# A fixed instruction order for four engines in the delta rule's products, with head norms summed in pairs

## The chip, the cores and the metric

The kernel runs on one core of a Trainium2 chip. Its engines are TensorE (PE, with its weight loads shown as PEld), VectorE (DVE), ScalarE (ACT), GpSimd (POOL) and SyncE (SP), which only issues DMAs here. The metric is the device time of one execution in microseconds (us), lower is better. The median of three runs of the kernel before is 2903.06 us (2902.81 to 2907.43).

## The reference

A block of three layers on 128 sequences of 32 tokens, width 512, in float32: `x = x + cross_attention(layernorm(x))`, then a delta-rule layer, then a feed-forward layer with Hadamard rotations and quantised weights. The change lies in the delta-rule layer, which computes per sequence:

```python
h = rms(layernorm(x), attn_norm_w)
q, k, v = (silu(silu(causal_dwconv(h @ W.T, conv))) for each)    # 4 taps along the tokens
q, k = l2norm(q), l2norm(k)                 # per head: 32 heads of 16
beta = sigmoid(h @ Wbeta.T)
for t in range(32):                         # the delta rule, S is 16x16 per head
    err = S @ k[t] - v[t]
    S = S - beta[t] * outer(err, k[t])
    o[t] = S @ q[t]
x = x + rms(o, out_norm_w) @ Wout.T
x = x + (silu(h2 @ Wgate.T) * (h2 @ Wup.T)) @ Wdown.T     # h2 = rms(x, mlp_norm_w)
```

The recurrence over 32 tokens is solved without a state: the products of all keys with all keys and queries of a sequence are formed first, a triangular system is solved by substitution over the tokens, and the result is multiplied by the masked query products.

## The kernel before

The program has four stages: cross attention; the **delta products** (`delta_products`); the **MLP stage** (`delta_out_mlp`), which finishes the delta layer and does its MLP; and the last feed-forward layer.

`delta_products` works in eight **rounds**, one per group of 512 rows (16 sequences). A round has twelve **steps** (`j` = 0 to 11): `k` and `q` for each of four 128-channel pieces in turn, then `v` for the four pieces. The last round goes through `k`, then `v`, then `q`.

In every step `channels` lets PE multiply the normed rows `hT` (transposed) with 128 columns of a weight into the PSUM bank `pp` (three of them), ACT scales it with the last tap into `acc` (three), and DVE adds the other three taps. One step later `activated` lets ACT apply Silu twice into `kq` or `v2`. The rest of a round is spread over the steps:

- `square` and `add`: squares of `k` and `q` (ACT), summed per head on PE into `sums` with the 0/1 matrix `hs`. `add` also multiplies `hT` with `wb` for the logits of beta.
- `lengths`: ACT takes Tanh and Sqrt of `sums`. In the next round `by_tokens` (step 1) turns them on PE, and DVE makes the norms `n` and `beta`; `put_q` and the `inverted` steps write the query norms (`rq`); `put_v` (steps 2 to 5) turns `v2` on PE, scales it on DVE into `vt` and writes it (`vd`).
- `products`: for each **piece** (128 channels by 256 rows; eight in a round) SP first loads `kqm`, a copy of `k` and `q` masked by head, with eight DMAs (`masked_operand`, three buffers, `hold` decides when). `multiply` then does sixteen small matmuls into two `pg` banks, ACT copies them to `kk` (six buffers), POOL writes `ld`, multiplies with the causal mask and writes `pd`. `due` lists the steps in which a piece is multiplied.
- `load`, `normed`: the next round's rows (`xt`, three buffers) are loaded, normed on DVE to `hn` (two buffers) and turned by PE and ACT into the next `hT`.

**Substitution** (`Substitution.solve`) works on the groups that are finished: DVE alternates a product `pr` and a subtraction from `W`, 31 times with falling length, 128 x 1984 elements at first. It loads `L` (one buffer, four loads) and `W` (two buffers) on SP and writes `ud` on POOL. `mixed` interleaves its steps with a round's by costs: a solve counts 90, `LANDING` (8) of it for the loads, and each round from the second gets `SHARE` (0.27 of a solve); the rest runs beside the MLP stage.

The order of instructions on PE and ACT is fixed in this stage to the order in which the program issues them, by the wrapper `InOrder`, which ties each instruction to the one before. DVE, SP and POOL are ordered by the scheduler, which may move a ready instruction ahead of others.

Ahead of round 0, `scaled_rows` multiplies the rows of `wk`, `wq`, `wv` and `wb` with `norm_w` on DVE, and POOL clears the operands `um` and `pe` that the MLP stage fills later. DVE clears `kqm` in the first steps.

Of the kernel before, what the change touches and what calls it, by code (L numbers as in the profile page):

```python
# [494 lines left out]
def scaled_rows(nc, wp, name, norm, ws, engine=None):  # L495

    mul = engine.mul if engine else nc.vector.tensor_scalar_mul
    nw = wp.tile([P, DC], FP, name=name, bufs=1)
    nc.sync.dma_start(nw, norm.rearrange("(c p) -> p c", p=P))
    for t in ws:  # L500
        for dc in range(DC):
            mul(t[:, dc, :], t[:, dc, :], nw[:, dc : dc + 1])


class Substitution:
# [4 lines left out]
    def __init__(self, g, pool, ld, vd, ud):  # L510
        self.nc, self.pool, self.ld, self.vd, self.ud = g.nc, pool, ld, vd, ud

    def solve(self, gi):
# [5 lines left out]
        def load(s):  # L519
            nc.sync.dma_start(  # L520
                L[:, s : s + some].rearrange("p s h t -> p s (h t)"), rows[:, s : s + some]
            )
# [3 lines left out]
        nc.sync.dma_start(  # L526
# [5 lines left out]
        for s in range(T):  # L532
            if s % some == 0 and s + some < T:
                load(s + some)
            nc.vector.tensor_mul(w[:, s], w[:, s], bc(W[:, s, :, HD], HD))
            n = T - 1 - s
            if n:
                pr = self.pool.tile([P, T - 1, H4, HD], FP, name="pr")
                nc.vector.tensor_mul(  # L539
                    pr[:, 0:n],  # L540
                    bc(L[:, s, :, s + 1 : T].rearrange("p h t -> p t h"), HD),
                    w[:, s].unsqueeze(1).to_broadcast([P, n, H4, HD]),
                )
                yield 0.3 + 0.07 * n
                nc.vector.tensor_sub(w[:, s + 1 :], w[:, s + 1 :], pr[:, 0:n])  # L545
# [7 lines left out]
def masked_operand(nc, m, kq):  # L553


    for h in range(HH):
        rows = slice(h * HD, (h + 1) * HD)
        nc.sync.dma_start(m[rows, h % H4], kq[rows])  # L558
# [31 lines left out]
def inverted(nc, rq, r):  # L590
# [3 lines left out]
    nc.sync.dma_start(r, every)  # L594
    yield
    nc.vector.tensor_scalar_max(r, r, 1e-12)
    nc.vector.reciprocal(r, r)
# [4 lines left out]
def delta_products(  # L602
    g: Ctx, x1, stats, norm_w, wqT, wkT, wvT, conv_q, conv_k, conv_v, wbT, heads, causal, ld, vd,
    pd, rq, kd, beside,
# [16 lines left out]
    act = InOrder(tc, nc.scalar)  # L621
    with stack:
# [13 lines left out]
        scaled_rows(nc, wp, "nw", norm_w, [w["k"], w["q"], w["v"], w["b"]])  # L636

        kqm = [wp3.tile([P, H4, 2, KT], FP, name=f"kqm{i}") for i in range(3)]
        blank = [t[:, h] for t in kqm for h in range(H4)]
        mv, rs = stats  # L640

        def load(n):
            xt = xp.tile([P, D], FP, name="xt")
            nc.sync.dma_start(xt, x1[n * P : (n + 1) * P, :])
            return xt

        def normed(n, xt, hT):

            i = n % GT
            hn = hp.tile([P, D], FP, name="hn")  # L650
            nc.vector.tensor_scalar(
                hn, xt, mv[:, n, 0:1], rs[:, n, 1:2], ALU.subtract, ALU.mult
            )
            act.copy(hT[:, :, i * P : (i + 1) * P], g.transposed(ps, hn, g.ident, pe=pe))

        def channels(hT, n, ec):
# [9 lines left out]
            for d in range(1, TAPS):  # L666
                last = nc.vector.scalar_tensor_tensor(  # L667
# [3 lines left out]
            return acc.rearrange("p b t -> p (b t)"), last.ins  # L671
# [16 lines left out]
        def hold():  # L688
            while len(held) < min(len(pieces), count["done"] + len(kqm)):
                gi, ec, half, kq = pieces[len(held)]  # L690
                m = kqm[len(held) % len(kqm)]
                masked_operand(nc, m, kq[:, :, half * KT : (half + 1) * KT])
# [13 lines left out]
        class Group:  # L706

            def __init__(self, gi):  # L710
                self.gi = gi
                self.sums = psn.tile([3 * H, SG], FP, name="pn")
                self.v = {}

            def square(self, kq, of="kq"):
# [3 lines left out]
                return sq  # L719

            def add(self, sq, hT, ec, of="kq"):
                at = dict(start=ec == 0, stop=ec == DC - 1)
                if "k" in of:
                    pe.matmul(self.sums[0:H], hs[:, ec, :], sq[:, 0], **at)
                    pe.matmul(
                        self.sums[H : 2 * H], w["b"][:, ec, :], hT[:, ec, :], **at
                    )
                if "q" in of:
                    return pe.matmul(self.sums[2 * H :], hs[:, ec, :], sq[:, 1], **at)

            def lengths(self, of="kq"):

                if "k" in of:
                    f = self.factors = wk.tile([3 * H, SG], FP, name="f", bufs=1)
                    act.activation(f[H : 2 * H], self.sums[H : 2 * H], AF.Tanh, scale=0.5)
                for n, r in (("k", slice(0, H)), ("q", slice(2 * H, 3 * H))):
                    if n in of:
                        act.activation(self.factors[r], self.sums[r], AF.Sqrt)

            def by_tokens(self):  # L740
                f = self.factors
                pt = ps.tile([P, GT, 2 * H], FP, name="ps")
                for i in range(GT):
                    pe.transpose(
                        pt[:, i, :], f[0 : 2 * H, i * P : (i + 1) * P], g.ident[0 : 2 * H, 0 : 2 * H]
                    )
                self.n = st.tile([P, GT, H], FP, name="n")
                nc.vector.tensor_scalar_max(self.n, pt[:, :, 0:H], 1e-12)
                self.beta = st.tile([P, GT, H], FP, name="beta")
                nc.vector.tensor_scalar(self.beta, pt[:, :, H:], 0.5, 0.5, ALU.mult, ALU.add)  # L750
                n2 = st.tile([P, GT, H], FP, name="n2", bufs=1)
                nc.vector.tensor_mul(n2, self.n, self.n)
                nc.vector.reciprocal(n2, n2)
                nc.vector.tensor_mul(self.beta, self.beta, n2)

            def put_q(self):

                for c in range(DC):
                    rows = slice(2 * H + c * HH, 2 * H + (c + 1) * HH)
# [5 lines left out]
            def put_v(self, ec):  # L765
# [6 lines left out]
                nc.vector.tensor_mul(  # L772
# [13 lines left out]
        def behind_round(old, j):  # L786
# [4 lines left out]
            if j == 1:  # L791
# [3 lines left out]
                    nc, rq[old.gi], st.tile([P, P], FP, name="rl", bufs=1)  # L795
# [9 lines left out]
        due = (0, 1, 1, 0, 1, 1, 0, 1, 1, 0, 1, 1)  # L805
        loads = (2, 3, 4, 8)
# [813 lines left out]
```

## Time and profile before

| | |
|---|---|
| median of 3 runs | 2903.06 us |
| the profiled execution | 2912.17 us |
| its span, first to last instruction | 2910.4 us |
| PE busy | 2815.8 us (97%) |
| DVE busy | 1995.4 us (69%) |
| ACT busy | 1034.9 us (36%) |
| POOL busy | 741.5 us (25%) |
| first `pp` matmul of the delta products | at 686.3 us |
| first `pm` matmul of the MLP stage | at 1215.7 us |

The first rows are device times; the others come from one profiled execution, whose own time is the one to set beside its span. Busy time is a union over an engine's instructions. PE's matmuls are pipelined, so a busy PE need not be at its peak rate; the granted clock (1.00 is full speed) is given beside it in the views by stretch. In the view of waits a line names the waiting engine, tile and line, what released it, the total in us, how often, and the longest. In a timeline a line has start, length, engine, source line, operation and count; the bracket is the idle time before it and what ended it. Helper calls through `InOrder` all stand under L151. Most fp32 matmuls show as two records.

### The profile page before, as it was taken

The numbers are of one execution on the slowest core, as the hardware profiler recorded it, in microseconds if no ns is written. First come the engines' busy times: TensorE is split into PE (matmuls) and PEld (weight loads), VectorE is DVE, ScalarE is ACT, GpSimd is POOL, SyncE is SP. The second block draws the span as 40 slices with busy tenths as digits, with TensorE's granted clock in tenths as the row PEclk, the third lists the DMA queues.
The fourth block names the chain that finished last, engine by engine and source line by source line (L and its number), as shares of the span: only waits on it lengthen the run. The fifth ranks groups of instructions, "written<-read, shape, count | busy, mean of one in ns | idle before, by whom it ended". The sixth has DMA issues, their size and how long they took to land.

```text
span 2910.4 us, 44713 instructions
## 1 busy us (share of the span) xinstructions
PE 2815.8 (97%) x16726; PEld 1676.1 (58%) x16726; DVE 1995.4 (69%) x3355; ACT 1034.9 (36%) x1794; POOL 741.5 (25%) x1102
## 2 busy tenths in 40 slices
PE   8999999997999899999999999999999999999998
PEld 4444444443434344567666767776776756666665
DVE  2453544425599895678787878887722279999997
ACT  1111111213666466522212221211221147677665
POOL 2232323322777677221212111101000000000000
PEclk9999999998999899999999999999999999999999
DMA  9898998873555545841414141413231124444443
GB/s 317 268 321 296 345 334 291 302 248 87 163 161 144 167 135 155 236 137 57 131 57 132 57 132 54 123 59 94 69 112 33 35 73 83 90 88 82 87 81 71
DMA packets 347176, 429.77 MB, mean 148 GB/s; under 512 B 151888, under 2 KB 252624, under 8 KB 344528
## 3 DMA queue, kind: packets, MB, share of 16 engines
q1 hardware_dynamic: 305952, 324.36, 37.0%
q0 software_dynamic: 41008, 102.55, 11.6%
q8 instruction: 133, 2.18, 0.3%
q14 instruction: 83, 0.68, 0.1%
HBM read 288.88 MB, written 94.37 MB: 132 GB/s over the span
## 4 chain that ended last, share of the span: by engine, by line
PE 58%; DVE 11%; issue 2%; DMA 2%; POOL 2%; ACT 1%; SPq 1%; ACTq 0%; DVEq 0%; POOLq 0%
PE ps L151 18%; PE pm L1063 9%; PE pm L1052 9%; PE pm L1055 9%; PE pp L151 4%; PE ps L1026 4%; DVE W L545 3%; DVE acc L667 2%; DVE pr L539 2%; PE ps L995 2%; PE pg L151 1%; POOL kk L583 1%; DMA xs<-x 1%; SPq L558 1%; PE pn L151 1%
## 5 line engine op out<-in xcount | busy, mean ns | idle before, releaser
L1052 PE MATMUL pm<-hT,wg 128*128 128x256 f32 x1408 | 341.1, 385 | 0.2 <-ACT hT L1041 0.2
L1055 PE MATMUL pm<-hT,wu 128*128 128x256 f32 x1408 | 336.4, 382 | 1.8 <-DVE wu L1113 1.3
L539 DVE TENSOR_TENSOR pr<-L,W 128x1984 f32<-128x1984 f32 (+30 forms) x248 | 307.6, 1240 | 8.6 <-DMA L<-ld 4.0
L545 DVE TENSOR_TENSOR W<-W,pr 128x1984 f32<-128x1984 f32 (+30 forms) x248 | 308.1, 1242 | 2.9
L1063 PE MATMUL pm<-wd,mT 128*128 128x512 f32 x704 | 307.4, 592 | 0.0
L1055 PEld LDWEIGHTS pm<-hT,wu 128*128 128x128 f32 x1408 | 269.3, 192 | 39.7 <-DVE wu L1113 1.6
L1052 PEld LDWEIGHTS pm<-hT,wg 128*128 128x128 f32 x1408 | 261.9, 190 | 50.0 <-issue 12.0
L1063 PEld LDWEIGHTS pm<-wd,mT 128*128 128x128 f32 x704 | 132.4, 190 | 160.2 <-issue 160.0
L151 PE MATMUL ps<-wq,qT 128*128 128x512 bf16 x960 | 217.1, 379 | 3.0 <-ACT t L151 3.0
L1057 ACT ACTIVATE sg<-pm 128x256 f32<-128x256 f32 x176 | 67.0, 382 | 325.3 <-PE pm L1052 311.8
L1058 DVE TENSOR_TENSOR mT<-pm,sg 128x256 f32<-128x256 f32 x176 | 73.8, 419 | 156.4 <-PE pm L1055 152.0
L1389 POOL DMA_DIRECT2D xo<-x x31 | 26.3, 849 | 526.1 <-ACT xo L151 491.7
L323 POOL DMA_DIRECT2D vx<-vn x256 | 126.3, 500 | 119.5 <-DVE vn L319 84.3
L151 PEld LDWEIGHTS <-qT 128*128 128x128 bf16 x960 | 94.0, 98 | 103.7 <-issue 3.9
L151 DVE TENSOR_TENSOR mb<-m 128x1024 f32<-128x1024 f32 x128 | 153.2, 1217 | 0.1
L151 DVE TENSOR_TENSOR m<-mb 128x1024 f32<-128x1024 f32 x128 | 150.7, 1219 | 1.2
L579 POOL DMA_DIRECT2D ld<-kk x128 | 93.4, 729 | 151.2 <-ACT kk L151 121.4
L151 ACT ACTIVATE t<-ps,magic,qs 128x512 f32<-128x512 f32 x158 | 115.5, 780 | 46.0 <-DVE qs L151 42.2
L583 POOL TENSOR_TENSOR kk<-kk,cm 128x256 f32<-128x256 f32 x128 | 124.9, 976 | 2.7
L151 PEld LDWEIGHTS ps<-hd,mT 128*128 128x128 f32 x1024 | 120.8, 194 | 6.9 <-ACT mT L151 2.8
L151 PE MATMUL pp<-hT,wk 128*128 128x512 f32 x256 | 122.3, 622 | 1.5 <-DVE acc L667 0.8
L151 PE MATMUL ps<-hd,mT 128*128 128x128 f32 x1024 | 121.3, 277 | 2.3 <-ACT mT L151 2.3
(230 smaller groups left out, 4820.0 us busy)
## 6 DMA issues: line engine op xcount, KB each, us to landing
kall<-in_ctxT_dram SPq DMA_DIRECT2D x32, 2056.0 KB
cx<-in_ctx_dram SPq DMA_DIRECT2D x32, 2048.0 KB
x<-xo POOLq DMA_DIRECT2D x64, 256.0 KB, 3.5
ld<-kk POOLq DMA_DIRECT2D x128, 128.0 KB, 2.6
pd<-kk POOLq DMA_DIRECT2D x128, 128.0 KB, 2.6
L<-ld SPq DMA_DIRECT2D x32, 512.0 KB
pe<-pd SPq DMA_DIRECT2D x256, 64.0 KB
kqm<-kq SPq DMA_DIRECT2D x448, 32.0 KB
```

Of the source, the lines that this page charges most:

```text
L151: got = method(*args, **kw)
L323: nc.gpsimd.dma_start(vx[r : r + T, j, :], vn[j * T : (j + 1) * T, halves[h]])
L539: nc.vector.tensor_mul(pr[:, 0:n], bc(L[:, s, :, s + 1 : T].rearrange("p h t -> p t h"), HD), w[:, s].unsqueeze(1).to_broadcast([P, n, H4, ...
L545: nc.vector.tensor_sub(w[:, s + 1 :], w[:, s + 1 :], pr[:, 0:n])
L579: nc.gpsimd.dma_start(ld[r].rearrange("(i p) f -> p i f", p=P), kk[:, 0].rearrange("p i h t -> p i (h t)"))
L583: nc.gpsimd.tensor_mul(q, q, cm.unsqueeze(1).to_broadcast([P, 2 * H4, T]))
L1026: nc.tensor.matmul(pw, oT[:, i, dc, :], wo[:, dc, :], start=dc == 0, stop=dc == DC - 1)
L1052: nc.tensor.matmul(pg, wg[:, dc, fs], hT[:, dc, :], start=dc == 0, stop=dc == DC - 1)
L1055: nc.tensor.matmul(pu, wu[:, dc, fs], hT[:, dc, :], start=dc == 0, stop=dc == DC - 1)
L1057: nc.scalar.activation(sg, pg, AF.Silu)
L1058: mark[:] = [nc.vector.tensor_mul(mT[:, fc, :], pu, sg).ins]
L1063: nc.tensor.matmul(pd, mT[:, fc, i * P : (i + 1) * P], wd[:, fc, :], start=fc == 0, stop=fc == FC - 1,)
```

## The change

- DVE and SP are wrapped in `InOrder` as well for this stage, so that their instructions, those of the substitution included, run in the order in which the program issues them. POOL is still ordered by the scheduler.
- Within a step `multiply` comes before `activated`, and `due` is shifted by one, so that a piece is multiplied a step later (in round 0 from step 5 on). `normed` goes a step ahead of the transposes, now `turned`; the fourth `xt` is loaded in step 7 instead of 8.
- The sums of squares go into four blocks of 32 rows instead of two: `add` runs twice a round (steps 6 and 10) on two channel pieces at once, one block for each of `k`, `q` and the piece's parity. The logits have a bank and a matmul group of their own (`logits`, 16 matmuls of 128 columns in step 11), and Tanh a tile of its own.
- The four tiles of round 0 are normed and turned before the weights are scaled; `wq` is scaled on ACT.
- `um` and `pe` are cleared on DVE in the first steps of round 0, in twelve pieces after those of `kqm`.
- The last round gets 0.7 of a share of substitution, at the pace of the others, so that its last part has none; `by_tokens` and `put_v` come a step later there.

```diff
-        scaled_rows(nc, wp, "nw", norm_w, [w["k"], w["q"], w["v"], w["b"]])
+    dve = substitution.dve = InOrder(tc, nc.vector)
+    sync = substitution.sync = InOrder(tc, nc.sync)
...
-        blank = [t[:, h] for t in kqm for h in range(H4)]
+        blank = [t[:, h] for t in kqm for h in range(H4)] + blanks
...
+            def add(self, ec, of="kq"):
+                if ec == 0 and "k" in of:
+                    self.sums = psn.tile([4 * H, SG], FP, name="pn")
+                for n in of:
+                    for r in range(2):
+                        at = (2 * "kq".index(n) + r) * H
+                        last = pe.matmul(
+                            self.sums[at : at + H], hs[:, ec + r, :], self.sq[r][:, "kq".index(n)],
+                            start=ec == 0, stop=ec == DC - 2,
+                        )
+                self.sq.clear()
+                return last
+
+            def logits(self, hT):
+                pb = ps.tile([P, P], FP, name="ps")
+                for dc in range(DC):
+                    for i in range(GT):
+                        pe.matmul(
+                            pb[i * H : (i + 1) * H], w["b"][:, dc, :], hT[:, dc, i * P : (i + 1) * P],
+                            start=dc == 0, stop=dc == DC - 1,
+                        )
+                self.tanh = st.tile([P, P], FP, name="tanh")
+                act.activation(self.tanh, pb, AF.Tanh, scale=0.5)
...
-        due = (0, 1, 1, 0, 1, 1, 0, 1, 1, 0, 1, 1)
-        loads = (2, 3, 4, 8)
+        due = (1, 0, 1, 1, 0, 1, 1, 0, 1, 1, 0, 1)
+        loads = (2, 3, 4, 7)
...
-                acc, last = channels(hT, n, ec)
-                with tc.issue_after(last):
-                    for _ in range(min(H4, len(blank))):
-                        nc.vector.memset(blank.pop(0), 0.0)
+                acc = channels(hT, n, ec)
+                for _ in range(min(H4, len(blank))):
+                    dve.memset(blank.pop(0), 0.0)
+                if due[j] and count["done"] < len(held) and (old or j >= 5):
+                    multiply()
                 activated()
                 waiting.append((acc, dst, masked(ec) if n == "q" else kept))
-                if due[j] and count["done"] < len(held) and (old or j >= 4):
-                    multiply()
                 if 3 <= j <= 9 and j % 2:
-                    sq = new.square(kq[(j - 3) // 2])
-                if 4 <= j <= 10 and j % 2 == 0:
-                    new.add(sq, hT, (j - 4) // 2)
+                    new.square(kq[(j - 3) // 2])
+                if j in (6, 10):
+                    new.add((j - 6) // 2)
...
                 if j == 11:
+                    new.logits(hT)
                     new.lengths()
                 if 7 <= j <= 10:
-                    normed((gi + 1) * GT + j - 7, xt[j - 7], hT_next)
+                    turned((gi + 1) * GT + j - 7, hn, hT_next)
+                if 6 <= j <= 9:
+                    hn = normed((gi + 1) * GT + j - 6, xt[j - 6])
...
         for i in range(GT):
-            normed(i, load(i), hT)
+            turned(i, normed(i, load(i)), hT)
+        for n, mul in (
+            ("k", dve.tensor_scalar_mul), ("b", dve.tensor_scalar_mul), ("q", act.mul),
+            ("v", dve.tensor_scalar_mul),
+        ):
+            scaled_rows(mul, w[n], nw)
...
-        for t in (*um, *pe):
-            nc.gpsimd.memset(t, 0.0)
...
-            return [(SHARE, part(all_u, SHARE))] if gi else []
+            return [(SHARE, part(all_u, SHARE * (0.7 if gi == NG - 1 else 1.0)))] if gi else []
```

## The prediction

> **What bounds the kernel now.** I read the page, then the busy time by stretch, which cuts the span into cross attention (0 to 686.3 us), the delta products (686.3 to 1215.7), the MLP stage (to about 2340) and the last FFN. The diff touches only the second. Cutting it at the first `pp<-hT,wk` of each round gives rounds 1 to 6 below (columns: stretch, length, then busy us of PE, PEld, DVE, ACT, POOL, granted clock, DMA share, GB/s).
>
> ```profile
> 744.60:805.90 61.30, 59.26 (x421) 25.55 (x413) 39.48 (x55) 39.49 (x65) 41.92 (x62) 1.00 0.60 171
> 805.90:870.80 64.90, 62.50 (x416) 26.73 (x412) 64.80 (x78) 40.31 (x66) 54.17 (x66) 0.97 0.57 157
> 870.80:936.70 65.90, 63.30 (x417) 26.75 (x413) 65.52 (x93) 40.55 (x66) 49.24 (x66) 0.97 0.53 148
> 936.70:1016.40 79.70, 64.59 (x417) 27.52 (x413) 71.44 (x98) 40.47 (x66) 54.11 (x67) 0.89 0.55 163
> 1016.40:1080.90 64.50, 60.88 (x417) 25.90 (x413) 61.74 (x83) 40.19 (x66) 49.77 (x66) 1.00 0.51 138
> 1080.90:1139.60 58.70, 58.70 (x416) 25.49 (x412) 33.10 (x52) 39.94 (x66) 47.33 (x70) 1.00 0.54 147
> ```
>
> All six do the same matmuls. Round 6 is pure PE: 58.7 us, no wait. Rounds 2 and 3 are pure DVE (64.80 of 64.90), because the substitution ran there as early as it could: by the same view its three lines take 6.9, 36.3, 37.8, 42.6, 33.0 and 0 us in rounds 1 to 6. So DVE is overfull in four rounds and half empty in the sixth. The six take 395.0 us against 6 x 58.7 = 352.2. The waits of the stage show how PE feels it:
>
> ```profile
> PEld pg L151 <- ACT kk L151: 31.0, 28, 4.2
> PE pg L151 <- ACT kk L151: 14.5, 13, 3.3
> PE pg L151 <- DMA kqm<-kq: 11.9, 2, 10.6
> PE ps L151 <- DVE hn L651: 9.9, 1, 9.9
> ```
>
> The PE timeline shows what a wait costs beyond itself: after 2.04 us the next eight `pp` records take 5.40 us (3.60 in round 6).
>
> ```profile
> 804.41 1.55 PE L151 MATMUL pg<-kqm,kq 64*32 64x256 f32 x32 [2.04 <-ACT kk L151]
> 805.90 5.40 PE L151 MATMUL pp<-hT,wk 128*128 128x512 f32 x8
> 974.47 2.82 PE L151 MATMUL pg<-kqm,kq 64*32 64x256 f32 x32 [10.55 <-DMA kqm<-kq]
> ```
>
> The 10.55 us in round 4 is SP's queue: a `W` load for a later group waits until 963.32 with the `kqm` loads behind it.
>
> ```profile
> 952.74 1.33 SPq L520 DMA_DIRECT2D L<-ld  x2
> 963.32 0.32 SPq L526 DMA_DIRECT2D W<-vd  x1
> 963.75 36.67 SPq L558 DMA_DIRECT2D kqm<-kq  x47
> ```
>
> At the front, DVE scales 16 weight pieces before the last two `hn`, slowed to 1.2 us each for `wq` while POOL's memset runs:
>
> ```profile
> 676.00 4.91 DVE L502 TENSOR_SCALAR wq<-wq,nw 128x512 f32<-128x512 f32 x4
> 682.99 0.99 DVE L651 TENSOR_SCALAR hn<-xt,mv,rs 128x512 f32<-128x512 f32 x2
> ```
>
> ```profile
> 675.76 4.08 POOL L1528 MEMSET pe<- 128x2048 f32 x2 [0.43 <-DVE mv L82]
> ```
>
> **The front.** The new order puts `hn` ahead of the scaling, gives `wq` to ACT and the memsets to DVE in round 0. PE's transposes of the first two tiles end at 673.8, which frees their buffers; two `hn` at 0.5 and the last statistics end near 674.5, four `wk` at 0.45 near 676.3. ACT's copies stand behind its table load and two square roots (to 676.3), two at 0.55 end at 677.4. First `pp` near 677.6 instead of 686.3: **-8.7**. Four `wq` on ACT, unseen there, cost between 0.48 (DVE's own) and 0.93 (ACT on 128x768); I take 0.6, 2.4 in all, done at 680 before the first `pp` ends (5.5 us, slow clock as now).
>
> **PE per round.** Before, `add` ran four times: six records (three column groups side by side) in 0.99 us each, so three matmuls cost hardly more than one. After, two times four groups: 1.98 if the fourth also runs beside the others, 3.7 if it does not; I take 1.98, since `ps<-pe,um` (128x32 weights in four groups) does 16 matmuls of 128 columns in 1.01. That row has the shape of `logits`, so 1.01 for it (2.0 if they ran singly, by the transposes' 0.49 for four). The `tanh` transpose adds 0.12. Net 3.96 to 3.11: -0.85, round 6's 58.7 becomes **57.9**.
>
> **DVE per round.** Other work than substitution is 28 to 29 us when DVE is full (64.8 - 36.3 in round 2). The written order spreads substitution over 71 steps, from step 9 of round 1 to step 8 of round 7. Of 156.6 us now, 0.3 of a share leaves (7.3 of 142 cost units, 8 us): 148.5 / 71 = 2.1 a step, 25 a round. With 0.2 to 0.3 for the split `n` (0.28 the whole), 54 us against PE's 57.9. The twelve new memsets (0.485, as the `kqm` ones) fall in round 0, where DVE has 31 of 58 busy; six steps there hold 1.9 of convolution and 1.9 of memset against PE's 3.44, some 2 us of lag, which the `pp` banks cover. ACT loses about 0.9 a round (three 0.59 rows become one and a shorter one).
>
> **The waits.** ACT's `kk` copies now stand before the two Silus of the step; at 933.39 ACT waited 4.26 for `acc` and the copies behind it released PE at 935.21. In the new order they need no convolution newer than two steps. `kqm` has three steps (14 us) instead of two (9.7) for two loads of 8 x 0.59 = 9.4. The early `W` load now comes a round after the `ud` write it waits for. So most of the 47.6 (395.0 - 6 x 57.9) can go. What the fixed queues add: on DVE, convolution 10 of round 1 stands behind the first `W` product, which waits for a load (landing 9.0 us; now 51 us into the round, DVE is there after nine steps of 4.8, one `pp` of 3.44 and 2.6 for `acc` and convolution, 49), some 2 us, which PE's three `pp` banks (14 us) absorb; on SP, `kqm` loads stand behind the second solve's `L` load, which waits for DVE to finish the first, at most a step's DVE work (5 us), again within three steps. I leave 1 us a round, bounds 0 (round 6 now) and 4 (rounds 2, 3, 5 now exceed 58.7 by 6 to 7, mostly DVE): rounds 1 to 6 become 353.4, **-41.6**. POOL: 47.3 without substitution, mean 51.8 with 37.4 of it, so near 50.
>
> **Round 0**: 1.33 of `kqm` wait gone, one product (1.02) moved to the end, `add` and `logits` -0.97: **-3.3**. **Round 7 and the tail** (76.1 to the first `pm`): +1.0 for that product, `add` 4 x 0.98 to 2 x 0.98 plus 1.1, the late `q` sums from four turns to two (-1.9); -1.7 in sum, but `wu`'s load waits on `put_q` there, so **-1**. Bounds 0 and -3. DVE has 46 us busy in these 76 and gets 17 more, none of it in the last third.
>
> **MLP stage**: PE 1113.6 of 1124.3. Substitution ends its second solve about 7.5 us later; its `um` copies end at 1264.9 for matmuls at 1286.9, so it is covered; without that slack up to 3 us. Taken at 0.
>
> Sum: -8.7 - 3.3 - 41.6 - 1 = -54.6. The profiled execution took 2912.17 (span 2910.4), so 2857.6; the median 2903.06 lies 9.1 below it, so 2848.5, say **2849**.
>
> **A rule against it.** POOL's `kk` multiply takes 0.74 alone and up to 2.75; in round 2, full of substitution, 17 took 20.17 us, in round 6 18 took 13.36. The Trainium skill, "SBUF — State Buffer", Who interferes with whom, says that a DVE instruction with two SBUF inputs shuts out a GpSimd instruction that reads SBUF, and the one that starts second waits for all of it. The rows of rounds 2 and 6 agree. By that rule a substitution product in nearly every step could catch nearly every multiply; it gives the third rival.
>
> **Rivals.**
> - *Strict order couples DVE and PE* (or DVE's 54 is really 61): each step waits a little, rounds of 62 rather than 58.9. For it: 93% load and no freedom to fill a gap. Against: three `pp` and `acc` buffers. 6 x 62 = 372, -23 - 13 = -36: 2867. Chance 0.25.
> - *SP's order stalls PE anyway*: loads behind `L`, `W` or `xt` come late some four times, 10.55 each: 42 back, 2891. The later use speaks against it. Chance 0.07.
> - *Slower*: every `kk` multiply is shut out as at worst. Then POOL has 47.3 + 16 x 2.0 = 79 us a round, `kk`'s six buffers fill, and PE waits: 6 x 79 - 395 - 13 = +66, 2969. It decides above (67.9 - 47.3)/16 = 1.29 over 0.74, a mean of 2.0 us; the densest round shows 1.19. With any mix of it and the second rival beyond 55 us of stalls: chance 0.07.
> - *It doesn't do what it says*: fewer matmuls save nothing as they overlapped already. Partly true, and counted; without it -48, 2856, inside the main case.
>
> **Chances.** Main case 0.59, coupling 0.25, SP 0.07, slower 0.07, no change 0.02. The main case alone runs from 2838 (no wait left, tail at its best) to 2860; the range adds the coupling case and its neighbours: 2836 to 2879. A measurement of this kernel can tell about 0.2% (5.8 us) from no change. Faster 0.91, same 0.02, slower 0.07.
>
> **What would show it.** First `pp` near 677.6; rounds 1 to 6 each 58 to 60 us, DVE busy evenly near 54; `pg <- kk` under 10 us and no `kqm` wait above 2; two `pn` groups of 1.0 and one `ps<-hT,wb` of 1.0 a round; MLP stage unchanged. Rounds above 62 with PE waiting for `acc` or `pp` would prove me wrong on DVE, `kk` multiplies near 2 us on POOL.

## The result and the profile after

The changed kernel takes 2875.2 us (median of 4 runs, 2874.1 to 2880.2) against 2905.2 for the kernel before on the same chip (2902.8 to 2911.0): a ratio of 0.9891, 95% interval 0.9876 to 0.9906. So it is 30 us faster where 54.6 were forecast. The profiled execution took 2874.5 us, its span is 2872.8. Cut as in the prediction:

| stretch | before | after | difference | forecast |
|---|---|---|---|---|
| up to the first transposes of the delta products | 672.7 | 667.1 | -5.6 | 0 |
| front: from there to the first `pp` | 13.6 | 4.5 | -9.1 | -8.7 |
| round 0 | 58.3 | 53.6 | -4.7 | -3.3 |
| rounds 1 to 6 | 395.0 | 370.6 | -24.4 | -41.6 |
| round 7 and the tail, to the first `pm` of L1083 | 76.0 | 81.4 | +5.4 | -1 |
| what follows | 1694.7 | 1695.6 | +0.9 | 0 |

The first row is work that the change does not touch; it lay between 665.8 and 672.7 in the profiles of this study. Without it the spans differ by 32.0 us, or 1.1%, as the medians do. Two rows carry the miss: rounds 1 to 6 (17.2 us less gain than forecast) and the tail (6.4 the other way).

Rounds 1 to 7 after, by the busy time by stretch (stretch, length, busy us of PE, PEld, DVE, ACT, POOL, granted clock, DMA share, GB/s):

```profile
725.20:790.00 64.80, 60.97 (x441) 27.27 (x437) 35.92 (x55) 39.83 (x65) 43.65 (x64) 0.95 0.58 167
790.00:850.90 60.90, 58.48 (x442) 25.89 (x438) 58.83 (x69) 39.82 (x65) 51.89 (x66) 1.00 0.52 145
850.90:911.60 60.70, 58.40 (x441) 25.88 (x437) 59.41 (x75) 39.97 (x65) 49.22 (x65) 1.00 0.56 153
911.60:975.70 64.10, 61.28 (x442) 27.19 (x438) 62.40 (x87) 40.06 (x65) 47.95 (x65) 0.95 0.53 144
975.70:1035.90 60.20, 59.23 (x442) 26.36 (x438) 53.83 (x80) 39.76 (x65) 44.98 (x67) 1.00 0.69 207
1035.90:1095.80 59.90, 58.35 (x442) 25.86 (x438) 57.51 (x71) 39.82 (x65) 51.05 (x65) 1.00 0.61 173
1095.80:1177.20 81.40, 73.33 (x453) 34.35 (x449) 70.85 (x103) 51.23 (x84) 50.69 (x73) 0.97 0.72 204
```

The rounds are even now, but none is at the pace of 57.9 that the prediction worked out for PE. DVE is busy for 97% of rounds 2 to 4 (58.83 of 60.90, 59.41 of 60.70, 62.40 of 64.10), not for 93%, and for 70.85 us of the tail's 81.4 where it had 46.0 before. The view of waits for this stage shows what became of PE's waits:

```profile
PE ps L151 <- DVE hn L151: 9.9, 11, 2.8
PE ps L97 <- DVE y L1071: 4.8, 1, 4.8
PE ps L151 <- DVE W L151: 3.8, 1, 3.8
```

The lines `pg <- ACT kk` (14.5 us) and `pg <- DMA kqm` (11.9) are gone from PE. What stands there instead is `hn`: the transposes of the next group's tiles in steps 7 to 10 wait for VectorE. The `W` line is one of them too, its releaser being the instruction just ahead of `hn`. The PE timeline has the two largest, and what follows each:

```profile
781.12 1.09 PE L151 MATMUL ps<-ident,hn 128*128 128x128 f32 x4 [3.83 <-DVE W L151]
782.00 6.05 PE L151 MATMUL pp<-hT,wv 128*128 128x512 f32 x8
...
951.54 1.11 PE L151 MATMUL ps<-ident,hn 128*128 128x128 f32 x4 [2.82 <-DVE hn L151]
952.45 6.16 PE L151 MATMUL pp<-hT,wv 128*128 128x512 f32 x8
```

The eight `pp` records behind each of them take over 6 us instead of 3.60, and the granted clock of these two rounds is 0.95. In round 1 that comes on top of the wait; in round 4 it cost nothing, as a run further down shows. In round 1, DVE in turn waited for the tile's load, and SP shows why: the load of `xt` stands in the written order behind the first solve's `L` and `W`, and the tile was there 8.5 us after its issue.

```profile
780.43 0.55 DVE L151 TENSOR_SCALAR hn<-xt,mv,rs 128x512 f32<-128x512 f32 x1 [6.19 <-DMA xt<-x]
```

```profile
769.72 0.39 SPq L151 DMA_DIRECT2D L<-ld  x1
770.32 1.52 SPq L151 DMA_DIRECT2D W<-vd  x1
771.93 0.44 SPq L151 DMA_DIRECT2D xt<-x  x1
```

### The profile page after: what moved, and what is told of

Same layout as the page of the kernel before. It is cut to its first block, busy times and chain, and to the rows that moved or that the text cites. A ratio compares the mean times of both kernels' runs of the same rounds, so it can differ in the third digit from the quotient of the medians.

```text
span 2872.8 us, 45044 instructions
## 1 busy us (share of the span) xinstructions
PE 2793.6 (97%) x16863; PEld 1675.9 (58%) x16926; DVE 2016.4 (70%) x3371; ACT 1037.3 (36%) x1791; POOL 728.4 (25%) x1098
## 4 chain that ended last, share of the span: by engine, by line
PE 59%; DVE 13%; issue 2%; DMA 1%; SPq 0%; ACT 0%; POOL 0%; DVEq 0%; POOLq 0%; ACTq 0%
PE ps L151 19%; PE pm L1083 10%; PE pm L1086 9%; PE pm L1094 9%; PE pp L151 5%; PE ps L1057 4%; DVE acc L151 3%; PE ps L1026 2%; DVE W L151 2%; DVE pr L535 1%; DVE W L541 1%; DVE pr L151 1%; PE pg L151 1%; DMA xs<-x 1%; DVE m L151 1%
## 5 line engine op out<-in xcount | busy, mean ns | idle before, releaser
L1083 PE MATMUL pm<-hT,wg 128*128 128x256 f32 x1408 | 342.5, 385 | 0.2 <-ACT hT L1072 0.2
L1083 PEld LDWEIGHTS pm<-hT,wg 128*128 128x128 f32 x1408 | 262.5, 191 | 50.3 <-issue 10.0
L535 DVE TENSOR_TENSOR pr<-L,W 128x960 f32<-128x960 f32 (+30 forms) x201 | 238.4, 1186 | 7.6 <-DMA L<-ld 3.8
L541 DVE TENSOR_TENSOR W<-W,pr 128x1024 f32<-128x1024 f32 (+30 forms) x202 | 241.3, 1195 | 2.3
L151 PE MATMUL ps<-wq,qT 128*128 128x512 bf16 x930 | 217.2, 381 | 4.6 <-ACT t L151 3.0
L151 PEld LDWEIGHTS <-qT 128*128 128x128 bf16 x960 | 94.4, 98 | 105.0 <-issue 6.1
L151 DVE TENSOR_TENSOR mb<-m 128x1024 f32<-128x1024 f32 x128 | 153.3, 1219 | 0.1
L151 DVE TENSOR_TENSOR m<-mb 128x1024 f32<-128x1024 f32 x128 | 150.8, 1220 | 1.2
L151 ACT ACTIVATE t<-ps,magic,qs 128x512 f32<-128x512 f32 x158 | 115.6, 780 | 42.7 <-DVE qs L151 38.9
L151 PEld LDWEIGHTS ps<-hd,mT 128*128 128x128 f32 x1024 | 120.8, 194 | 6.9 <-ACT mT L151 2.8
L151 PE MATMUL ps<-hd,mT 128*128 128x128 f32 x1024 | 121.3, 277 | 2.3 <-ACT mT L151 2.3
L151 PE MATMUL pp<-hT,wv 128*128 128x512 f32 x256 | 120.3, 614 | 0.0
L579 POOL TENSOR_TENSOR kk<-kk,cm 128x256 f32<-128x256 f32 x128 | 118.4, 925 | 2.7
L151 PE MATMUL pp<-hT,wk 128*128 128x512 f32 x256 | 116.2, 596 | 1.9 <-ACT hT L151 1.9
```

Source lines behind the costliest of these rows:

```text
L151: got = method(*args, **kw)
L535: self.dve.tensor_mul(pr[:, 0:n], bc(L[:, s, :, s + 1 : T].rearrange("p h t -> p t h"), HD), w[:, s].unsqueeze(1).to_broadcast([P, n, H4, ...
L541: self.dve.tensor_sub(w[:, s + 1 :], w[:, s + 1 :], pr[:, 0:n])
L579: nc.gpsimd.tensor_mul(q, q, cm.unsqueeze(1).to_broadcast([P, 2 * H4, T]))
L1083: nc.tensor.matmul(pg, wg[:, dc, fs], hT[:, dc, :], start=dc == 0, stop=dc == DC - 1)
```

## The experiments

The question was where 17 us of rounds 1 to 6 and 6 us of the tail went. Theory A: the order. `hn` stands in DVE's written order only one step ahead of the transposes that need it, behind a step's convolution and substitution, so PE waits as soon as DVE is a step late. The main rival, called B and later G: DVE simply has too much to do, and a wait removed at `hn` comes back elsewhere. Each run has a ratio to the kernel before on the same chip; their intervals are about 0.2% to either side, so small effects are read from the profiles by stretch.

**Rows three steps ahead, and the loads alone.** Both kernels load at steps 1 to 4 and normalise in place in one pool of five buffers; only the first norms earlier too.

```diff
-        loads = (2, 3, 4, 7)
+        loads = (1, 2, 3, 4)
...
-                    turned((gi + 1) * GT + j - 7, hn, hT_next)
-                if 6 <= j <= 9:
-                    hn = normed((gi + 1) * GT + j - 6, xt[j - 6])
+                    turned((gi + 1) * GT + j - 7, hn.pop(0), hT_next)
+                if 4 <= j <= 7:
+                    hn.append(normed((gi + 1) * GT + j - 4, xt[j - 4]))
```

> The changed kernel with the normalised rows three steps ahead: loads at steps 1 to 4, `normed` at steps 4 to 7 (in place in the loaded rows, five buffers in one pool instead of three and two), the turned transposes left at 7 to 10. Theory A (rounds 1 to 6 lose their 23 us over the pace of TensorE because `hn` stands in DVE's fixed order only one step ahead of its transposes): the waits of the turned transposes for `hn` (9.9 us in 11) go to under 2 us, the six rounds shrink from 370.6 to 352 to 358 us, time 2855 to 2863 against 2875.2. Rival B (DVE itself has too little room in these rounds, so that the wait only moves to the convolution's `pp` and `acc`): the waits for `hn` go but others of the same size come, six rounds 366 to 372, time 2871 to 2878. Rival C (the late load of the fourth rows alone): as the next kernel, 2866 to 2871.

> As the kernel above in loads and buffers (loads at steps 1 to 4, in place, five buffers), but `normed` left at steps 6 to 9, one step ahead of the transposes. Theory A: only the two waits of `hn` for `xt` (7.5 us, 6.2 of them in round 1) go; round 1 from 64.8 to 60 to 62, the other rounds within 1 us each; time 2869 to 2873. Rival C (the load alone makes the loss): the six rounds fall to 352 to 358, time 2855 to 2863. Rival B: no change, 2873 to 2877.

Rows ahead: 2873.6 us, ratio 0.9897 (0.9878 to 0.9916). Rounds 1 to 6 take 363.5, 7.1 less than in the changed kernel; rounds 1 and 6 are at 58.05. The time does not show these 7 us: in this execution the stage started 4 us later, the front took 0.9 more and the rest 1.1. The waits for `hn` are gone, and the view of waits names what came for them:

```profile
ACT acc L151 <- DVE acc L151: 69.2, 46, 4.3
PE pn L151 <- ACT sq L151: 6.8, 5, 2.3
```

The first line was 22.2 us in 15 in the changed kernel. ScalarE's Silus now wait for the convolution, the squares stand behind the Silus, and `pn` behind the squares. So A is right on the wait that PE had, and B on what is behind it: between the two forecasts.

The loads alone: 2872.4 us, 0.9894 (0.9877 to 0.9912). Round 1 falls from 64.8 to 58.05, as the SP lines said, but round 2 rises from 60.9 to 63.75 with a 3.78 us wait for `hn`; the six rounds are 366.2. The late load cost round 1 its 6.9 us over the pace; a part of that went on to the next round. So 4.4 of the 7.1 us come with the earlier loads, and the earlier place of `hn` adds only 2.7. In rounds 2 to 4 it gave nothing: the rows ahead take 186.1 us there, the changed kernel 185.7.

**VectorE left to the scheduler.**

```diff
-    dve = substitution.dve = InOrder(tc, nc.vector)
+    dve = substitution.dve = nc.vector
```

> The changed kernel with VectorE's order left to the scheduler (one line), the other three laid out. Theory A (it is the laid-out order that holds `hn` behind the substitution): the waits for `hn` fall below 4 us, but front and tail give some back; time 2858 to 2872. Rival B (DVE has too little room whatever its order): 2872 to 2885. Rival D (the laid-out DVE order is what the gain over the kernel before comes from): the waits of TensorE for `hn` and for DVE grow, 2885 to 2905.

2892.3 us, 0.9958 (0.9945 to 0.9972): inside rival D's range. Rounds 1 to 6 go back to 391.4, with 66.1, 73.5 and 66.9 us in the worst three, and PE's waits for `hn` grow:

```profile
PE ps L151 <- DVE hn L649: 15.5, 7, 5.7
```

So without the laid-out order of VectorE 20.8 of the 24.4 us in the rounds are lost. A part of that is work that moved: the scheduler ran all of the substitution ahead of the tail, 153.0 us of it in rounds 1 to 6 instead of 133.6, and the tail is shorter for it, 75.8 us instead of 81.4. Rounds and tail together lose 15.2 us. The substitution comes in bunches again: VectorE is busy for 73.0 us in round 3 and for 41.5 in round 4.

**The last round's old steps.**

```diff
-                if j == 9:
+                if j == 8:
                     new.by_tokens()
-                if j >= 10:
-                    for ec in range(2 * (j - 10), 2 * (j - 9)):
-                        new.put_v(ec)
-                        left["pool"].append(left["vt"])
+                if j >= 9:
+                    new.put_v(j - 9)
+                    left["pool"].append(left["vt"])
+                if j == 11:
+                    new.put_v(DC - 1)
```

> The changed kernel with the last round's factors and values at their old steps: `by_tokens` at step 8, `put_v` one each at steps 9 and 10 and two at 11, instead of 9, 10 twice, 11 twice. Theory E (this delay by a step is what makes the stretch from the last round's start to the first `pm` 5.3 us longer than before): that stretch falls from 81.4 to 75 to 78 us, the rest the same; time 2869 to 2873. Rival F (the laid-out DVE order and the share of the substitution make it): the stretch stays at 80 to 83, time 2873 to 2878.

2873.9 us, 0.9897 (0.9882 to 0.9912); the tail takes 79.8 us instead of 81.4. That is less than theory E said: the step's delay accounts for 1.6 of 5.4 us at most. Even that is not shown, since the tail of the kernel with the loads alone, which has the last round of the changed kernel, took 79.9.

**Less substitution in the rounds.**

```diff
-            return [(SHARE, part(all_u, SHARE * (0.7 if gi == NG - 1 else 1.0)))] if gi else []
+            return [(SHARE, part(all_u, SHARE * (0.7 if gi == NG - 1 else 0.8)))] if gi else []
...
-                return [(PACE, part(all_u, PACE))]
+                pace = PACE + (15.0 if b < 2 else 0.0)
+                return [(pace, part(all_u, pace))]
```

> The changed kernel with the substitution's share in rounds 1 to 6 at 0.8 of what it was (0.7 in the last round as before), and its pace in the first two blocks of the MLP stage raised from 45 to 60 so that each group is solved before it is read. Theory G (the leftover 23 us of rounds 1 to 6 come from VectorE's load: 58.8, 59.4 and 62.4 us busy in rounds 2 to 4 against TensorE's pace of 57.9): VectorE falls by about 5 us a round to 54 to 57, rounds 1 to 6 from 370.6 to 354 to 361, the MLP stage longer by 0 to 4; time 2858 to 2868 against 2875.2. Rival A (the laid-out order alone, whatever the load): rounds 366 to 371, time 2871 to 2876. Rival H (the MLP stage gives it all back): rounds 354 to 361 and the MLP stage longer by over 8, time 2872 or more.

2893.2 us, 0.9930 (0.9910 to 0.9949): every forecast missed. VectorE did fall, to 55.0, 56.3 and 55.8 us in rounds 2 to 4, and yet these three took 61.3, 62.7 and 61.2 us, 185.2 in sum against 185.7. PE's waits for `hn` did not go (17.6 us against 9.9 and the 3.8 under `W`; the longest, 4.7, is again the late `xt` of round 1, and 3.3 is new in round 5):

```profile
PE ps L151 <- DVE hn L151: 17.6, 11, 4.7
PE pg L151 <- DMA kqm<-kq: 6.3, 1, 6.3
```

So in these three rounds less load without another place for `hn` is worth nothing, against theory G taken alone. Rounds 5 and 6 took 64.6 and 68.9; the second line, in round 6, is an old acquaintance from the kernel before, as SP shows:

```profile
1050.84 1.92 SPq L518 DMA_DIRECT2D L<-ld  x2
1062.91 0.32 SPq L522 DMA_DIRECT2D W<-vd  x1
1063.34 14.50 SPq L151 DMA_DIRECT2D kqm<-kq  x16
```

L518 and L522 (without `InOrder`'s L151) are loads of a solve that belongs to the MLP stage, outside the written order. The scheduler drew them into round 6, where SP stood for 10 us with the `kqm` loads behind. This is the prediction's second rival; in the changed kernel itself no `kqm` wait on PE is left.

**The rows normalised on ScalarE.**

```diff
-            dve.tensor_scalar(hn, xt, mv[:, n, 0:1], rs[:, n, 1:2], ALU.subtract, ALU.mult)
+            act.activation(xt, xt, AF.Identity, bias=nb[:, n : n + 1], scale=rs[:, n, 1:2])
```

> The kernel with the rows three steps ahead, with the normalisation itself moved from VectorE to ScalarE (one activation with scale and bias a tile; VectorE makes the 32 biases in two small instructions). Theory G: VectorE loses 2.5 to 4.5 us a round, ScalarE gains 2 to 3 and stays below 44 of 60; rounds 1 to 6 at 352 to 358 us, time 2858 to 2866. Rival I (ScalarE's fixed order, where the Silus wait for the convolution, is what now makes TensorE wait for the squares): rounds 361 to 366 as with the rows ahead alone, time 2869 to 2875.

2875.0 us, 0.9864 (0.9844 to 0.9884). The view by stretch of rounds 1 to 5:

```profile
733.10:791.10 58.00, 58.00 (x441) 25.96 (x437) 30.63 (x47) 42.36 (x69) 43.68 (x64) 1.00 0.63 177
791.10:849.20 58.10, 58.10 (x443) 25.97 (x438) 56.94 (x67) 42.47 (x69) 52.22 (x64) 1.00 0.58 159
849.20:907.20 58.00, 58.00 (x441) 25.97 (x437) 56.71 (x72) 42.34 (x69) 53.00 (x68) 1.00 0.60 163
907.20:968.40 61.20, 60.21 (x445) 26.26 (x438) 59.53 (x81) 42.42 (x69) 46.77 (x64) 1.00 0.55 152
968.40:1033.00 64.60, 61.49 (x441) 27.32 (x437) 54.79 (x82) 42.83 (x69) 49.42 (x67) 0.95 0.66 195
```

Rounds 1 to 3 and 6 are pure PE at 58.05 us. VectorE has 56.9 us instead of the 59.6 of the kernel with the rows ahead, and the wait of `pn` falls from 6.8 to 0.9. The two theories can be compared in rounds 2 to 4: 185.7 us in the changed kernel, 186.1 with the rows ahead alone, 185.2 with less load alone, 177.2 with both. So neither is worth anything there without the other. It fits that 59.6 us of work on VectorE have no room in a round of 58.05, and 56.9 have. (The edit also takes `hn` out of VectorE's order altogether, so load and order are not fully separated.) The time hides the gain, because the front grew to 9.2 us (four tiles of 0.80 us wait on ScalarE behind its queue) and the stretch after the first `pm` took 5.8 us more, 1701.4; in the runs that left the MLP stage as it was, it lay between 1694.4 and 1701.4. Round 5 lost 3.11 us, and the slow matmuls after, to `kqm`.

**The pieces as before.**

```diff
+        due = (0, 1, 1, 0, 1, 1, 0, 1, 1, 0, 1, 1)
...
-                if due[j] and count["done"] < len(held) and (old or j >= 5):
-                    multiply()
                 activated()
                 waiting.append((acc, dst, masked(ec) if n == "q" else kept))
+                if due[j] and count["done"] < len(held) and (old or j >= 4):
+                    multiply()
```

> The changed kernel with the pieces of the masked products a step earlier and behind the two Silus of their step, as before the change (both the list of steps and the place in the step, in the last round too); the four laid-out orders stay. Theory J (that move took away the waits of TensorE for `kk` and `kqm`): the `pg <- kk` waits come back with 10 to 30 us, rounds 1 to 6 from 370.6 to 382 to 395, time 2886 to 2898. Rival K (the laid-out orders alone took them away): rounds 368 to 374, time 2873 to 2878.

2890.7 us, 0.9922 (0.9902 to 0.9942). Rounds 1 to 6 take 376.5 (+5.9) and round 0 58.8 (+5.1, with one product and 1.7 us of a slower first `pp` in it). Round 5 alone makes the 5.9 (66.6 against 60.2). What came back is not `kk` but `kqm`, 5.28 us of it in round 5:

```profile
PE pg L151 <- DMA kqm<-kq: 9.9, 6, 5.3
```

So the piece's later step removed waits for its loads. The waits for `kk`, 14.5 us on PE before, stay away even with the old place, and they stayed away with VectorE left to the scheduler too, where the pieces were at the later step. Neither of the two is needed for it alone; which part of the change took them is not shown. The forecast of 382 to 395 was too high for that reason.

**No substitution in the last round** (rounds 1 to 6 as changed, pace 60 in the first two blocks of the MLP stage).

> The changed kernel without any substitution in the last round (rounds 1 to 6 keep their share; the pace in the first two blocks of the MLP stage 60 instead of 45). Theory F (the last round's VectorE load of 70.9 us of 81.4, 46.0 of 76.1 in the kernel before, makes the tail longer): the stretch from the last round's start to the first `pm` of the MLP falls from 81.4 to 74 to 77, the MLP stage longer by 0 to 3; time 2869 to 2873. Rival L (the order of the tail's own instructions makes it): the stretch stays at 79 to 82, time 2873 to 2878.

2884.6 us, 0.9906 (0.9889 to 0.9923). The tail falls to 75.0 us, as theory F said, with 52.0 us of VectorE instead of 70.9. But the rest takes 1708.6 us, 13 more than after, where 0 to 3 were expected. In the first MLP block, PE now waits for `um`, which is made from the substitution's result:

```profile
1260.69 3.70 PE L1026 MATMUL ps<-pe,um 128*32 128x128 f32 x64 [6.76 <-POOL um L1008]
```

The substitution's 23 us in the last round cost the tail 6.4 us; at this pace they cost more in the MLP stage.

Rounds 1 to 6 are those of the changed kernel, so this run also tells what slow matmuls cost. In round 4, PE waited 2.82 us for the same `hn`, but the `pp` records behind it were fast, and PE then stood again at the next `hn`:

```profile
953.91 3.60 PE L151 MATMUL pp<-hT,wv 128*128 128x512 f32 x8
960.66 0.66 PE L151 MATMUL ps<-ident,hn 128*128 128x128 f32 x4 [2.13 <-DVE hn L151]
```

The round took 63.9 us, against 64.1 with the slow records. VectorE, busy for 62 us of it, set its length either way.

**Towards a better version.** First, the ScalarE kernel with its front back on VectorE, and with the later solves' loads kept in SP's written order; then the same with the last round's old steps.

```diff
+            if n < GT:
+                dve.tensor_scalar(xt, xt, mv[:, n, 0:1], rs[:, n, 1:2], ALU.subtract, ALU.mult)
+            else:
+                act.activation(xt, xt, AF.Identity, bias=nb[:, n : n + 1], scale=rs[:, n, 1:2])
...
-    substitution.dve, substitution.sync = nc.vector, nc.sync
+    substitution.dve = nc.vector
```

> The kernel with the rows ahead and normalised on ScalarE, with two edits more: the four tiles of the front are normalised on VectorE as in the changed kernel, and the substitution's loads stay in SP's written order to the end, so that loads of the MLP stage's solves can't be drawn into the rounds ahead of `kqm` loads. Theory M (rounds 4 and 5 lost 3 and 6.6 us to `kqm` loads that stood behind such loads, and the front 4.7 us to ScalarE's queue): front 4.4 to 5.5, all six rounds 58.0 to 59.5 (348 to 356 in sum), time 2856 to 2865. Rival N (the `kqm` loads are late for another reason): round 5 stays at 63 to 65, time 2867 to 2872. Rival O (the later solves start late in the MLP stage): rounds as by theory M and the MLP stage and what follows 1700 or more, time 2864 to 2872.

> The kernel above with the last round's factors and values at their old steps (`by_tokens` at 8, `put_v` at 9, 10, 11 and 11). From the run of that edit alone (79.8 against 81.4 us from the last round's start to the first `pm`): 1 to 2 us below the kernel above, 2854 to 2864; no difference would say that the 1.6 us was chance.

2860.9 us, 0.9837 (0.9816 to 0.9857), and 2859.5 us, 0.9840 (0.9824 to 0.9855). Both intervals lie below that of the changed kernel (0.9876 to 0.9906). The front is 5.3, the six rounds 357.5 and 357.0, the tail 79.1 and 77.2. The second beats both kernels, by 1.6% the one before. Its tail is 1.9 us shorter than the first's, near the 1.6 us of the edit alone; neither this, within the scatter seen above, nor the times can tell the two apart. The times lie in theory M's range, but M was wrong on rounds 4 and 5: they stay at 61 to 63 us, close to what N said of round 5. The stretch after the first `pm` took 1701.1 us in the first, as O said, but 1694.4 in the second, which has the same MLP stage.

**The squares' sums a step later**, on the kernel with the rows ahead on VectorE.

```diff
-                if j in (6, 10):
-                    new.add((j - 6) // 2)
+                if j in (7, 11):
+                    new.add((j - 7) // 2)
```

> The kernel with the rows three steps ahead (VectorE normalises), with the sums of squares a step later (`add` at steps 7 and 11 instead of 6 and 10). Theory A (what is left of the loss there is order: TensorE's `pn` matmuls stand too close behind the squares, which stand behind the Silus and the convolution): the waits of `pn` for `sq` (6.8 us in 5 on PE) go, rounds 1 to 6 from 363.5 to 356 to 360, time 2866 to 2871. Theory G (what is left is VectorE's load, 59.6, 59.1 and 63.2 us in rounds 2 to 4): the wait moves on to another place, rounds 1 to 6 at 361 to 365, time 2871 to 2876.

2869.7 us, 0.9876 (0.9860 to 0.9892). The wait of `pn` is gone and three rounds take 57.9, but the six 363.9, as G said. The wait moved to the values' products in DVE's order, which hold PE's transposes:

```profile
PE ps L151 <- DVE vt L151: 5.1, 3, 2.7
```

**The next solve's loads later**, on the best kernel, for the loss that was left in round 5.

```diff
+        if gi:
+            yield 3.0
         load(0)
...
-        yield LANDING
+        yield LANDING - 3.0 if gi else LANDING
```

> The kernel above (rows ahead on ScalarE, substitution's loads in SP's written order, the last round's old steps) with the first loads of each solve but the first written 3 cost units (a step and a half) later; the allowance for their landing is shortened by as much, so the sum of the costs stays. Theory P (rounds 4 and 5 still lose 3 and 4.6 us because the second solve's `L` load stands in SP's order ahead of `kqm` loads and waits there for VectorE to finish the first solve, 968.5 to 977.8 us): round 5 falls from 62.6 to 58 to 60, the six from 357.0 to 351 to 355, time 2853 to 2859 against 2859.5. Rival Q (the wait stays with whatever is behind the load, or VectorE now waits for the late `W`): the six stay at 356 to 359, time 2858 to 2864.

2868.5 us, 0.9854 (0.9830 to 0.9879): nearer to rival Q than to theory P, but the six rounds took 361.4, above Q's range too. Round 5 rose to 66.4. SP stands idle until 983.82, 17.5 us into the round, though `L` is no longer ahead; in the kernel above its `kqm` loads started 17.6 us into round 5, so something other than `L` holds them until then (most likely the piece or its buffer; not shown). VectorE waited for the late `W` (12.33 us), and the next eight `kqm` loads, issued right behind `L`, `W` and an `xt`, took 13.04 us, the eight after them 5.08:

```profile
996.73 0.38 SPq L151 DMA_DIRECT2D L<-ld  x1
997.16 0.44 SPq L151 DMA_DIRECT2D W<-vd  x1
997.64 0.48 SPq L151 DMA_DIRECT2D xt<-x  x1
998.23 13.04 SPq L151 DMA_DIRECT2D kqm<-kq  x8
...
1012.00 5.08 SPq L151 DMA_DIRECT2D kqm<-kq  x8
```

Theory P had the wrong culprit: not `L`'s wait for a buffer, since the start did not move without it. Whether it is the traffic of a solve's loads stays open. Round 4 of the kernel above loses its 3.0 us at the two `pn` groups: the first takes 2.12 us instead of 1.06, the second 3.03 from its first matmul to its last, 0.92 of it a wait for `sq`. These are the squares behind the Silus and the convolution again, and VectorE is busy for 59.3 us in this round, more than the pace of 58.05.

## Why the prediction was right and wrong

The direction was right; two terms were mis-sized, the leftover waits of rounds 1 to 6 and the tail.

- **Front: right.** -9.1 for -8.7. The first `pp` waited 1.91 us for `hT` and ran at once at 3.70 instead of the slow 5.5 that was allowed, which is about what round 0 gained beyond the forecast (-4.7 for -3.3). That part was luck: in three runs with the same front and the same wait (old steps of the last round, less substitution, none in the last round) the first `pp` took 5.16 to 5.40, and round 0 took 55.1 to 55.3, as forecast.
- **PE's pace: right.** 57.9 us a round shows as 57.91 in three rounds of the kernel with the late sums and as 58.05 in others; two `pn` groups of 1.0 and one `ps<-hT,wb` of 1.0 to 1.1 a round, as assumed.
- **Waits for `kk` and `kqm`: right** in the changed kernel, where PE has none of either above 1 us. The causes were not as told: the later step removed `kqm`, and the waits for `kk` stay away without it.
- **"54 us against PE's 57.9": wrong, and it was the root.** Rounds 2 to 6 measured 58.8, 59.4, 62.4, 53.8 and 57.5. Two parts of the sum failed. "Other work than substitution is 28 to 29" took the substitution's busy time (36.3) from VectorE's (64.8) as if no two records overlapped. Round 2's busy times before, by tile, are 36.3 + 25.1 (convolution) + 2.2 (`hn`) + 5.0 (`n`, `vt`) + 1.2 (`rl`), or 69.7 us unrounded, so some 5 of them overlap and the other work is 33 us by itself. The changed round 2 has 58.83 - 26.58 = 32.3 of other work by the same subtraction, and round 6 before, which has no substitution to subtract, already said 33.1. And "25 a round" was spread by cost units, where rounds 2 to 6 had 26.6, 27.8, 30.4, 21.3 and 25.2. The 8 us that were to leave did not show either: fewer substitution instructions ahead of the MLP stage, 141 instead of 148, took 156.9 us against 156.7, because one takes longer on average now (the first 141 took 150.2 before; why is not shown).
- **"I leave 1 us a round": wrong.** 370.6 - 6 x 57.9 = 23.2 us were left, 17 more than the six forecast. The three `pp` banks were said to cover DVE's lag. They cover that of the convolution; the transposes of `hn` have no such cover, since `hn` is made one step earlier on a queue that is itself late. The prediction put no price on that, and none on the `xt` load behind `L` and `W`. Of the 23.2 us, 6.9 lie in round 1 and go with earlier loads, and 4.3 in rounds 5 and 6. The other 12.0 lie in rounds 2 to 4; 8.5 of them went when `hn` was made earlier and VectorE had less to do, in the kernel with the rows on ScalarE (-12.6 in all six rounds), and none with one of the two alone.
- **The rival "strict order couples DVE and PE (or DVE's 54 is really 61)"** is what happened: 372 us forecast for the six rounds, 370.6 measured. It had 0.25 and should have led. That the number fits so well is in part luck: 6.9 of the leftover come from the late `xt`, which this rival does not speak of, and PE waited for `hn`, not for `acc` or `pp`, as the prediction's sign of it said. It was written as one or the other; in rounds 2 to 4 the runs show that both hold, as neither less load nor an earlier `hn` gave anything alone.
- **"Against: no freedom to fill a gap":** strictness was a gain, not a loss. With VectorE free the rounds lose 20.8 us, and 15.2 together with the tail.
- **Tail "-1": wrong, +5.4.** "It gets 17 more, none of it in the last third" was costed at nothing. It got 24.8 more (70.85 for 46.03). With no share of the substitution the tail is 75.0 against 76.0 before, so the rest of the sum, -1, was right. The rest of that share is no gift either: the MLP's slack for `um`, taken as cover, is gone when the share moves there (6.76 us of wait, 13 in all).
- **The SP rival** occurred once and small in the changed kernel, and not at `kqm`: it is the `xt` load of round 1 behind `L` and `W`. Waits of PE for `kqm` came back in others (6.33, 5.28 and 3.73 us at the longest); in one of them SP shows the mechanism that the rival named.
- **The rule against it** (the Trainium skill, "SBUF — State Buffer", Who interferes with whom) cost TensorE nothing here: POOL's `kk` multiply has a mean of 907 ns over the stage against 959 before, and POOL stays below 52 us a round. The multiplies do get longer beside substitution (means of 1.02 to 1.03 us in rounds 2, 3 and 6, at worst 2.65, against 0.74 in round 1, which has little of it), but not always: round 5, with 21.3 us of it, has a mean of 0.76.

## What to carry to other kernels

Before a full engine is put into a written order, list for each of its results how many steps lie between its place and its reader; here the one with the fewest set the first waits, and the next in line took over when it was moved. Busy times by tile do not add up to an engine's busy time where records overlap, so check a load that comes from a subtraction against a stretch that has only one kind of its work. The busy share alone does not tell the bound: VectorE was busy for 97% of the changed kernel's rounds 2 to 4, and for 98% of rounds 2 and 3 with the rows on ScalarE, where PE never waited. Compare its work in us with the other engine's pace, and where the two are close, take work off it and move the early operand; one alone gave nothing here.

## What the runs showed of the hardware

Matmuls behind a wait of PE of some 2 to 4 us are often slower, but the length of the wait does not decide it. After 2.82 us in round 4 of the changed kernel the next eight `pp` records took 6.16 us instead of 3.60, with a granted clock of 0.63 in the 9 us from 951 on. In the runs with the old steps of the last round and without substitution there, waits of 2.81 and 2.82 us at the same place were followed by 3.60 us and a granted clock of 1.00. In the front, after 1.91 us, the first eight took 3.70 us in one run and 5.16 to 5.40 in four. Eight `kqm` loads that were issued right behind the loads of `L`, `W` and one `xt` took 13.04 us on SP in one run and 8.51 in round 1 of the changed kernel, and the eight after them 5.08 and 5.09. One activation with scale and bias of a 128x512 tile takes 0.80 us on ScalarE, against a mean of 0.79 for VectorE's instruction for the same work in the changed kernel (0.65 before, 0.52 at the shortest).
